# Layer 3 of a graph network: transposing node features on VectorE in 32 by 32 squares instead of on TensorE

## Chip, cores and metric

The kernel runs on one core of one Trainium2 chip. The metric is the time of one execution on the device in microseconds (us), the median of several runs. The core has five engines with a queue of instructions each: TensorE (PE in the profile; PEld is its loading of weights), VectorE (DVE), ScalarE (ACT), GpSimd (POOL) and SyncE (SP, here the queue that starts the loads). Each engine works its own queue in order; between engines, an instruction waits on semaphores for what it needs.

## What is computed

A stack of four layers over a graph of 3,327 nodes with 64 features each, and one weighted adjacency matrix of 3,327 by 3,327, all in fp32. Every layer normalizes, applies relu and adds its result to x. Cut to what matters here:

```python
# layer 0: two gated graph cells       (two products with adj)
# layer 1: ranks of non-zero entries   (one product with a matrix made from adj)
# layer 2: w = adj * adj, three hops   (three products with adj squared)
h = jnp.maximum(_layernorm(x, axis=-1), 0.0)
x = x + _L3_gnn_ref(h, adj, L3_gnn_W)          # layer 3

def _L3_gnn_ref(user_embs, adj, W):
    x = user_embs
    for k in range(2):
        agg = adj @ x
        x = jnp.tanh(jnp.concatenate([agg, x], axis=1) @ W[k])
    return x
```

So each of the two hops of layer 3 multiplies two things with weights: the sum over neighbours `agg`, and the node's own features `x` that the hop began with.

## The kernel before

**Layout.** The nodes are padded to 3,328 = 2 x 13 x 128: two halves `s`, 13 blocks `b` of 128 nodes. They are worked in four chunks of 3, 3, 3 and 4 blocks (both halves of each), and chunks go in two groups: (0, 1) and (2, 3). Features exist in two forms. In node form (`y[k][c]`, a tile of 128 partitions by blocks, halves and 64 features) the nodes lie on the partitions; this form is the stationary operand of the products with the adjacency. In feature form (`both[c]`, 128 partitions by 2 halves and blocks x 128 nodes) the features lie on the partitions. Of `both[c]`, half `s` holds on one set of 64 partitions the sum over neighbours and on the other set, `upper(1 - s)`, the node's own features, so that one matmul with 128 rows of weights does the concatenated product of the reference.

**Propagation.** There are eight products with the adjacency, k = 0 to 7; layer 3 is k = 6 and 7. A unit (k, c, t) takes one tile `t` of the transposed adjacency (128 source nodes by all targets of a group) and adds its part to the sum of chunk c in PSUM: two matmuls at L517, each with two records in the profile, so four. For k = 3, 4, 5 the tile is squared first, two of three by ScalarE (L360) and one of three by VectorE (L362). The tiles come from HBM into 20 slots on the SyncE queue (L325); a slot is loaded again when the last unit that uses its tile is done.

**Order.** The units are laid out in one list. `joint(g, k, ...)` runs products k and k + 1 of a group together, k + 1 some tiles behind; `alone` runs one. The end of the list is joint(1, 4), joint(0, 5), joint(1, 6), alone(0, 7). So source product 5 of chunks 2 and 3 ends in joint(1, 4), that of chunks 0 and 1 in joint(0, 5), and so on. `run` writes the units to the engines' queues in this order. Squares are issued up to three units before the unit that uses them (`EXPAND`).

**What comes between.** When the sum of a chunk is complete, its task starts: `after_5` to `after_7` in layer 3. A task is a Python generator. Each `yield us` says how much stream time should pass before its next part is put into the queues; `spend` counts that time down by 0.86 us per unit of 512 columns (0.645 us for 384). Each engine may run ahead of TensorE in its own queue as far as its data allow. If a chunk's next task begins, the rest of its old one is put out first (`finish`).

- `after_5(c)`: the sum of layer 2's last hop is copied (`evacuate`), multiplied with weights, added to x (L728), then layer norm and relu on VectorE with one power on GpSimd (L713 to L724). The result is y[6][c]. Then `transpose_to_features` puts the same features into `both[c]`.
- `after_6(c)`: `evacuate_stacked` copies the sum into the other half of `both[c]` (L704 on ScalarE, L705 on VectorE), `stacked_to_nodes` multiplies both parts with the weights (L677), tanh gives y[7][c], and `transpose_to_features` puts these into `both[c]` for the second hop.
- `after_7(c)`: the same without a transpose; the result is added to x and written out.

`transpose_to_features` takes a bank of PSUM, makes one matmul with the identity for each block and half (L694: 6 for three blocks and 8 for four; each stands in the profile as two records, so 12 and 16), and copies the bank out in two halves, here with `vector=True` one on ScalarE (L700) and one on VectorE (L698). It is also used once per chunk at the start, in `before_0`.

Of the kernel before, what the change touches and what calls it, by code (L numbers as in the profile page):

```python
# [44 lines left out]
N, D = 3327, 64  # L45
# [43 lines left out]
def upper(n):  # L89
    return slice(n * D, (n + 1) * D)  # L90
# [3 lines left out]
def kernel(  # L94
# [9 lines left out]
    nc = tc.nc  # L104
# [19 lines left out]
    both = [const.tile([P, 2, (b1 - b0) * P], F32, name=f"both{c}") for c, (b0, b1) in enumerate(CH)]  # L124
# [93 lines left out]
    def blocks(c):  # L218
        return CH[c][1] - CH[c][0]

    def width(c):
        return blocks(c) * P
# [15 lines left out]
    def take(sums=False, either=False):  # L238

        pool = idle_sums if sums else idle_temps  # L240
        if either and idle_sums and (not pool or released[idle_sums[0]] < released[pool[0]]):
            pool = idle_sums
        for c in list(tasks):
            if not pool and c not in running:
                advance(c)
        i = pool.popleft()
        return i, banks[i]

    def give(i):
        released[i] = max(released) + 1  # L250
        (idle_sums if i < 4 else idle_temps).append(i)

    def nodes(c):

        return feat.tile([P, blocks(c), 2, D], F32, name=f"y{c}")

    def flat(t):
        return t.rearrange("p b s d -> p b (s d)")
# [394 lines left out]
    def evacuate(acc, c, busy=False):  # L653
        m = work.tile([P, CWM], F32, name="t2")[:, :width(c)]
        if c % 2 or busy:
            nc.scalar.copy(m, acc[1][:, :width(c)])  # L656
        else:
            nc.vector.tensor_copy(m, acc[1][:, :width(c)])  # L658
        give(acc[0])
        return m  # L660

    def dense_to_nodes(ft, w, c):

        i, ps = take()
        v = view(ps, c)
        for b in range(blocks(c)):
            mm(v[:, b, :], ft[:, b * P:(b + 1) * P], bd[:, w - WL1, :])
        return i, v

    def stacked_to_nodes(c, w):  # L670

        i, ps = take()
        v = view(ps, c)
        for b in range(blocks(c)):
            for s in range(2):
                for n in range(2):
                    nc.tensor.matmul(v[upper(n), b, upper(s)], both[c][:, s, b * P + n * D:b * P + (n + 1) * D], w(s),  # L677
                                     start=True, stop=True)
        return i, v
# [7 lines left out]
                mm(v[:, b, upper(s)], ft[:, b * P:(b + 1) * P], ident[:, upper(1 - s)])  # L687
        return i, v

    def transpose_to_features(h, c, vector=False):  # L690
        i, ps = take()
        for b in range(blocks(c)):
            for s in range(2):
                nc.tensor.matmul(ps[upper(1 - s), b * P:(b + 1) * P], h[:, b, s, :], ident, start=True, stop=True)  # L694
        for s in range(2):
            u = upper(1 - s)
            if s and vector:
                nc.vector.tensor_copy(both[c][u, s], ps[u, :width(c)])  # L698
            else:
                nc.scalar.copy(both[c][u, s], ps[u, :width(c)])  # L700
        give(i)

    def evacuate_stacked(acc, c):
        nc.scalar.copy(both[c][upper(0), 0], acc[1][upper(0), :width(c)])  # L704
        nc.vector.tensor_copy(both[c][upper(1), 1], acc[1][upper(1), :width(c)])  # L705
        give(acc[0])

    def layernorm_relu(h, c, scale=None, pace=1.0):
        n = 2 * blocks(c)
        v = groups(xchunk(c))  # L710
        st = work.tile([P, 4, 8], F32, name="st", bufs=4)
        xc = work.tile([P, 8, D], F32, name="t2")
        nc.vector.tensor_reduce(st[:, 0, :n], v, AX.X, ALU.add)  # L713
        nc.vector.tensor_scalar(st[:, 1, :n], st[:, 0, :n], 1.0 / D, None, op0=ALU.mult)
        nc.vector.tensor_tensor(xc[:, :n], v, st[:, 1, :n, None].to_broadcast([P, n, D]), ALU.subtract)
        yield 1.5 * pace
        nc.vector.tensor_tensor(groups(h), xc[:, :n], xc[:, :n], ALU.mult)
        nc.vector.tensor_reduce(st[:, 2, :n], groups(h), AX.X, ALU.add)
        nc.vector.tensor_scalar(st[:, 2, :n], st[:, 2, :n], 1.0 / D, EPS, op0=ALU.mult, op1=ALU.add)  # L719
        nc.gpsimd.tensor_tensor(st[:, 3, :n], st[:, 2, :n], mhalf[:, :n], ALU.pow)  # L720
        yield 2.5 * pace
        if scale is not None:
            nc.vector.tensor_scalar(st[:, 3, :n], st[:, 3, :n], scale, None, op0=ALU.mult)
        nc.vector.scalar_tensor_tensor(groups(h), xc[:, :n], 0.0, st[:, 3, :n, None].to_broadcast([P, n, D]),  # L724
                                       op0=ALU.max, op1=ALU.mult)

    def residual(v, c):
        nc.vector.tensor_tensor(flat(xchunk(c)), flat(xchunk(c)), v[1], ALU.add)  # L728
        give(v[0])
# [73 lines left out]
    def before_0(c):  # L803
        h = nodes(c)
        yield from layernorm_relu(h, c)
        y[0][c] = h
        yield 12.0 + 3.0 * c
        transpose_to_features(h, c)
# [50 lines left out]
    def after_5(c, acc):  # L859
        m = evacuate(acc, c)  # L860
        yield 0.8
        v = dense_to_nodes(m, WL2 + 2, c)
        yield 0.8
        residual(v, c)
        yk = nodes(c)
        yield from layernorm_relu(yk, c)
        y[6][c] = yk
        yield 0.8
        transpose_to_features(yk, c, vector=True)

    def after_6(c, acc):
        evacuate_stacked(acc, c)
        yield 0.8
        v = stacked_to_nodes(c, lambda s: w3[:, 0, s])
        yk = nodes(c)
        nc.scalar.activation(flat(yk), v[1], AF.Tanh)
        give(v[0])
        y[7][c] = yk
        yield 1.2
        transpose_to_features(yk, c, vector=True)  # L880

    def after_7(c, acc):
        evacuate_stacked(acc, c)
# [8 lines left out]
        nc.scalar.dma_start(out=out[:, g0:g1], in_=xs[:, g0:g1])  # L892

    after[:] = [after_0, after_1, after_2, after_hop(3), after_hop(4), after_5, after_6, after_7]


# [60 lines left out]
```

## Time and profile before

| | |
|---|---|
| time, median of 3 runs (lowest, highest) | 737.91 us (737.57, 739.96) |
| span of the profiled execution | 734.9 us |
| read from HBM | 199.68 MB |
| granted clock of TensorE | 0.997 |
| products with the adjacency, fp32 (L517) | 2912 records, 536.0 us busy |
| squares on ScalarE (L360), on VectorE (L362) | 113.7 us, 69.4 us busy |

The busy time of an engine is the time in which at least one of its instructions ran. Matmuls overlap, so the mean length of one is more than the time by which the queue moves on; the step of the queue is seen in the chain of waits, where a run of matmuls stands with its start, its length and its count. The idle column of a group says how long the engine stood still just ahead of it, and for what.

### The profile page before, as it was taken

The page shows a single profiled execution, that of the slowest core. Times are in us where ns is not written, and L with a number is a line of the kernel's source. Part 1 is how long each engine was busy: PE and PEld are TensorE (multiplying, and loading weights), DVE is VectorE, ACT ScalarE, POOL GpSimd, SP SyncE. Part 2 cuts the span into 40 slices and gives each one's busy share as a digit, 9 for nine tenths or more (in the row PEclk, how much of TensorE's full clock was granted, in tenths as well). Part 3 has the DMA queues.
Part 4 walks back from the last instruction along what each step waited for, and adds up shares of the span by engine and source line. Part 5 has one row for each costly group of instructions (what it writes and reads, how often), then busy time and mean ns, then how long its engine had stood idle before and what let it go on. Part 6 is the DMA issues. An engine that isn't in the chain of part 4 may idle for free. (4 is left out here: it accounts for less than half of the span.)

```text
span 734.9 us, 12499 instructions
## 1 busy us (share of the span) xinstructions
PE 694.7 (95%) x5112; PEld 347.6 (47%) x5112; DVE 340.1 (46%) x599; ACT 244.6 (33%) x383; POOL 72.6 (10%) x105
## 2 busy tenths in 40 slices
PE   5988999899999898989899999999999999999997
PEld 2543566344546685545344444334344454344443
DVE  6656736434997978758764114321252520000101
ACT  0103100212037767768848213730044601000101
POOL 4100000001290502112200000000110000000000
PEclk9999999999999999999999999999999999999999
DMA  9999996189587365571799749953987399916991
GB/s 340 401 357 405 405 392 213 44 323 364 179 288 280 105 219 186 183 283 45 276 351 383 263 145 408 406 230 109 393 298 251 126 396 405 401 39 238 399 403 38
DMA packets 68964, 201.54 MB, mean 274 GB/s; under 512 B 7388, under 2 KB 8644, under 8 KB 68908
## 3 DMA queue, kind: packets, MB, share of 16 engines
q1 hardware_dynamic: 66156, 199.70, 73.2%
q8 instruction: 40, 0.66, 0.4%
q10 hardware_dynamic: 576, 0.85, 0.3%
q0 software_dynamic: 2176, 0.20, 0.2%
q14 instruction: 16, 0.13, 0.0%
HBM read 199.68 MB, written 0.85 MB: 273 GB/s over the span
## 5 line engine op out<-in xcount | busy, mean ns | idle before, releaser
L517 PE MATMUL sum<-adj,y 128*64 128x384 f32 (+1 forms) x2912 | 536.0, 516 | 17.8 <-DMA adj<-in_adjT 13.5
L517 PEld LDWEIGHTS sum<-adj,y 128*64 128x64 f32 x2912 | 218.4, 138 | 274.0 <-issue 230.3
L360 ACT ACTIVATE adj<-adj 128x768 f32<-128x768 f32 (+1 forms) x138 | 113.7, 891 | 57.7 <-PE sum L517 36.6
L383 DVE TENSOR_SCALAR adj<-adj 128x768 bf16<-128x768 f32 (+3 forms) x208 | 112.5, 593 | 33.5 <-PE temp L453 29.5
L362 DVE TENSOR_TENSOR adj<-adj 128x768 f32<-128x768 f32 (+1 forms) x70 | 69.4, 1022 | 57.1 <-DMA adj<-in_adjT 32.6
L433 ACT ACTIVATE e<-temp,bitsb 128x384 int16<-128x384 f32 (+1 forms) x123 | 68.8, 600 | 24.2 <-PE temp L229 18.4
L517 PE MATMUL sum<-e,adj 128*64 128x384 bf16 (+1 forms) x624 | 72.9, 339 | 0.0
L705 DVE COPY both<-sum 64x384 f32<-64x384 f32 (+1 forms) x16 | 9.5, 594 | 130.5 <-ACT both L704 130.5
L704 ACT COPY both<-sum 64x384 f32<-64x384 f32 (+1 forms) x16 | 8.0, 499 | 149.4 <-PE sum L517 149.4
L229 PE MATMUL temp<-adj,tri 128*64 128x384 bf16 (+1 forms) x320 | 49.6, 346 | 7.9 <-DMA adj<-totals 2.5
L720 POOL TENSOR_TENSOR st<-st,mhalf 128x6 f32<-128x6 f32 (+1 forms) x16 | 27.0, 1688 | 301.1 <-DVE st L719 292.6
L517 PEld LDWEIGHTS <-adj 128*64 128x64 bf16 x624 | 41.3, 110 | 17.2 <-issue 5.3
L388 POOL DMA_DIRECT2D adj<-totals x52 | 31.4, 606 | 134.6 <-DVE adj L768 74.7
L229 PEld LDWEIGHTS <-tri 128*64 128x64 bf16 x416 | 28.6, 111 | 29.2 <-issue 14.7
L431 DVE TENSOR_SCALAR e<-temp 128x512 int16<-128x512 f32 (+1 forms) x37 | 23.5, 634 | 20.5 <-PE temp L229 11.4
L748 PE MATMUL temp<-both,cells 128*64 128x384 f32 (+1 forms) x128 | 27.4, 521 | 4.1 <-DVE adj L757 2.2
L658 DVE COPY t<-sum 128x384 f32<-128x384 f32 x8 | 4.4, 556 | 54.3 <-PE sum L517 54.3
L453 PE MATMUL temp<-adj,behind 128*64 128x384 bf16 x208 | 28.6, 339 | 0.3 <-DVE adj L383 0.2
L656 ACT COPY t<-sum 128x384 f32<-128x384 f32 (+1 forms) x8 | 4.3, 533 | 67.0 <-PE sum L517 67.0
L700 ACT COPY both<-temp 64x384 f32<-64x384 f32 (+1 forms) x16 | 8.0, 502 | 55.5 <-PE temp L694 55.4
L453 PEld LDWEIGHTS <-behind 128*64 128x64 bf16 x208 | 16.2, 110 | 16.2 <-issue 14.4
L229 PE MATMUL sum<-adj,tri 128*64 128x384 bf16 (+1 forms) x96 | 17.4, 335 | 2.4 <-DVE e L431 2.4
(83 smaller groups left out, 293.5 us busy)
## 6 DMA issues: line engine op xcount, KB each, us to landing
adj<-in_adjT SPq DMA_DIRECT2D x130, 768.0 KB, 7.7
adj<-in_adjT SPq DMA_DIRECT2D x104, 896.0 KB, 11.6
xs<-in_x SPq DMA_DIRECT2D x1, 640.0 KB
out<-xs ACTq DMA_DIRECT2D x3, 192.0 KB, 1.9
adj<-totals POOLq DMA_DIRECT2D x26, 3.0 KB, 4.6
adj<-totals POOLq DMA_DIRECT2D x26, 3.5 KB, 2.2
folds<-in_weights SPq DMA_DIRECT2D x4, 64.0 KB, 11.8
out<-xs ACTq DMA_DIRECT2D x1, 256.0 KB
```

Of the source, the lines that this page charges most:

```text
L229: nc.tensor.matmul(out[hs], lhsT[:, hs], rhs, start=start, stop=stop)
L360: nc.scalar.activation(sq, v, AF.Square)
L362: nc.vector.tensor_tensor(sq, v, v, ALU.mult)
L383: nc.vector.tensor_scalar(t.mask.view[:rows, half], t.view()[:rows, half], 0.0, None, op0=ALU.not_equal)
L388: nc.gpsimd.dma_start(out=t.mask.view[P - 1:P], in_=totals[t.g][t.q:t.q + D + 1:D, :])
L431: nc.vector.tensor_scalar(wide[:, s], ps[:, :w], BITS, 0.0, op0=ALU.add, op1=ALU.max)
L433: nc.scalar.activation(wide[:, s], ps[:, :w], AF.Relu, bias=bitsb)
L453: nc.tensor.matmul(counts[c][1][s * D:(s + 1) * D, :w], behind[:, NQ - 1 - t.q:NQ - 1 - t.q + D], t.mask.view[:, s, t.cols(c)], start=firs ...
L517: nc.tensor.matmul(acc[h * D:(h + 1) * D, :w], yq[h], rhs[h], start=first and n == 0, stop=last and n == len(terms) - 1)
L705: nc.vector.tensor_copy(both[c][upper(1), 1], acc[1][upper(1), :width(c)])
L720: nc.gpsimd.tensor_tensor(st[:, 3, :n], st[:, 2, :n], mhalf[:, :n], ALU.pow)
L748: nc.tensor.matmul(ps[upper(1 - s), :w], cells[:, cell, s, g, :], both[c][:, s], start=True, stop=True)
```

## The change

The features of layer 3 no longer pass through TensorE and PSUM on their way into `both[c]`. VectorE has an instruction that transposes squares of 32 by 32. The new `transpose_on_vector` uses it from the node form in SBUF straight to the feature form in SBUF: for each half `s`, each quarter `q` of 32 nodes of a block and each half `f` of the 64 features, one instruction takes 32 partitions and all blocks of the chunk (3 or 4 squares). That is 16 instructions per chunk, put into the queue four at a time with `yield 1.5` after each four. The `yield` ahead becomes 1.5 as well (0.8 in `after_5`, 1.2 in `after_6` before). The start of the kernel (`before_0`) keeps the old way, with both copies on ScalarE as before. The purpose is to take the transposes and their weight loads off TensorE, and the copies out of PSUM off ScalarE and VectorE.

```diff
-    def transpose_to_features(h, c, vector=False):
+    def transpose_to_features(h, c):
...
-            u = upper(1 - s)
-            if s and vector:
-                nc.vector.tensor_copy(both[c][u, s], ps[u, :width(c)])
-            else:
-                nc.scalar.copy(both[c][u, s], ps[u, :width(c)])
+            nc.scalar.copy(both[c][upper(1 - s), s], ps[upper(1 - s), :width(c)])
         give(i)
+
+    def transpose_on_vector(h, c):
+
+        for s in range(2):
+            to = both[c][:, s].rearrange("p (b q n) -> p b q n", q=4, n=32)
+            for q in range(4):
+                for f in range(2):
+                    at = (1 - s) * D + f * 32
+                    nc.vector.transpose(to[at:at + 32, :, q], h[q * 32:(q + 1) * 32, :, s, f * 32:(f + 1) * 32])
+                if q % 2:
+                    yield 1.5
...
         y[6][c] = yk
-        yield 0.8
-        transpose_to_features(yk, c, vector=True)
+        yield 1.5
+        yield from transpose_on_vector(yk, c)
...
         y[7][c] = yk
-        yield 1.2
-        transpose_to_features(yk, c, vector=True)
+        yield 1.5
+        yield from transpose_on_vector(yk, c)
```

## The prediction

> **What bounds the kernel now.** I read the page's busy shares first, then the chain that ended last, the timeline of TensorE and VectorE around the lines that change, and the waits.
>
> ```profile
> PE 694.7 (95%) x5112; PEld 347.6 (47%) x5112; DVE 340.1 (46%) x599; ACT 244.6 (33%) x383; POOL 72.6 (10%) x105
> ```
>
> ```profile
> 588.99 0.66 PE temp L694 x12
> 589.64 5.16 PE sum L517 x32
> 594.80 0.66 PE temp L694 x12
> 595.46 9.67 PE sum L517 x60
> ```
>
> TensorE (PE) is busy for 95% of the span (first fence, the page). In the chain (second fence: start, length, what) the transposes of L694 stand between the big matmuls of L517 with no gap on either side: twelve take 0.66 us of TensorE's queue. So in layer 3 TensorE's queue sets the time, and whatever leaves it ends the program sooner, unless something else arrives late.
>
> ```profile
> L694 PE MATMUL temp<-ident,y 128*64 128x128 f32 x104 | 7.1, 275 | 1.4 <-DVE y L724 1.4
> ...
> L698 DVE COPY both<-temp 64x384 f32<-64x384 f32 x6 | 3.3, 550 | 14.6 <-ACT both L700 14.5
> ```
>
> These are groups from 500 to 735 us, shapes kept apart: 104 records of transposes (two for each matmul, 8 visits of a chunk), with 1.4 us of TensorE standing idle in front of them, waiting for VectorE's last step of the layer norm. The record of one is 275 ns long, but they overlap; their step is 0.66/12 = 55 ns.
>
> ```profile
> 533.31 0.88 PE L694 MATMUL temp<-ident,y 128*64 128x128 f32 x12 [0.16 <-DVE y L724]
> ...
> 544.75 1.09 PE L694 MATMUL temp<-ident,y 128*64 128x128 f32 x16 [1.19 <-DVE y L724]
> ...
> 548.11 32.47 PE L517 MATMUL sum<-adj,y 128*64 128x384 f32 x200 [0.33 <-DVE adj L362]
> ```
>
> In TensorE's timeline the idle time sits before the transposes of chunks 2 and 3; after the second, TensorE waits 0.33 us for a square of the adjacency (L362). The reason is seen on VectorE:
>
> ```profile
> 544.01 0.69 DVE L724 SCALAR_TENSOR_TENSOR y<-t,st 128x512 f32<-128x512 f32 x1 [1.53 <-POOL st L720]
> 546.51 0.68 DVE L698 COPY both<-temp 64x512 f32<-64x512 f32 x1 [1.81 <-ACT both L700]
> 547.12 0.94 DVE L362 TENSOR_TENSOR adj<-adj 128x768 f32<-128x768 f32 x1
> ```
>
> The square at 547.12 stood in the queue behind the copy L698, which itself waited for TensorE and ScalarE.
>
> [...] No transpose by VectorE is in the trace of before[...]. [...] So I let the transposes pay their full length one after the other. [...]
>
> **Part by part.**
>
> *Removed from TensorE.* Six visits with three blocks (12 matmuls, 0.66 us each in the chain) and two with four blocks (16 matmuls, 0.88 us: "667.25 to 668.13"): 6 x 0.66 + 2 x 0.88 = 5.7 us. The wait in front of them, 0.16 + 1.19 = 1.35 us (1.4 in the group), goes too: what TensorE finds next are propagation units that don't need the new features. The square that came 0.33 us late is no longer behind L698. Sum: 7.1 us, all on the path.
>
> *Removed elsewhere.* Eight copies L700 on ScalarE (about 0.5 us), eight L698 on VectorE (6 x 0.55 + 2 x 0.68 = 4.7 us), and the PSUM bank taken for each. Neither engine is the bound; I count nothing.
>
> *Added on VectorE.* Per visit 2 (halves) x 4 (node quarters) x 2 (feature halves) = 16 transposes of 32 partitions by 96 elements (three blocks) or 128. Price: in the trace a VectorE step over 6 elements takes 172 ns (L719) and one over 384 takes 553 ns (L713); the straight line between them is 1.0 ns per element, so 96 elements give 262 ns and 128 give 294 ns. Lower end: 172 ns, the price of a step with almost no data. Upper end: streaming at half rate, 172 + 2 x 90 = 352 ns. I take 262 and 294. Sum: 96 x 0.262 + 32 x 0.294 = 34.6 us, against 4.7 removed. It is laid out in bursts of four (about 1.05 us), with 1.5 us of modelled stream between them.
>
> *Does it hide?* By stage:
> 1. Chunks 2 and 3 after source layer 5 (533 to 552 us). This is the tight place. From 533.3 to 546.5 VectorE has three squares (2.9 us), the layer norm of chunk 3 (4.5 us), and now 16 transposes of chunk 2 (4.2 us): 11.6 of 13.2 us. It fits, but a square may queue behind a burst. Four squares (three, and the one at 547) behind one burst each is at most 4 x 1.05 to 1.18, about 4.4 us, if TensorE needed each at once. But the squares are issued three units ahead (3 x 0.65 = 1.9 us), and before, a 3.3 us run of layer norm in that queue cost TensorE nothing. I take 1 us for all of them.
> 2. Chunks 0 and 1 (588 to 600 us). Last square at 582; the layer norm of chunk 1 may stand behind two bursts (2.1 us, less the 0.55 us copy), so its features come at about 595.6 instead of 594.07. TensorE needs them at about 600.0 (six units of 0.65 us before the sum that ends at 603.9), less the 1.3 us saved: 598.7. Hidden.
> 3. After source layer 6 (606 to 614 and 656 to 669 us). VectorE has nothing to do but the transposes and the copies L705. The first burst can run as soon as the tanh is there (606.4), ahead of the copy at 609.6; the others are queued behind it. Hidden, at most some tenths.
> 4. Who waits for the transposes: only the matmuls L677 of the next visit of that chunk, at 605, 610, 656, 665, 686, 694, 725 and 729 us, each at least 16 us after the features were ready. 16 x 0.29 = 4.7 us, plus three gaps, fits everywhere.
>
> *Transfers.* If TensorE is 7 us early, can the adjacency keep up? By windows of 5 us, the last loads end between 715 and 720:
>
> ```profile
> 710.00:715.00 5.00, 5.00 (x34) 2.17 (x32) 0.00 (x0) 0.00 (x0) 0.00 (x0) 1.00 1.03 402
> 715.00:720.00 5.00, 5.00 (x34) 2.28 (x32) 0.00 (x0) 0.00 (x0) 0.00 (x0) 1.00 0.46 178
> 720.00:725.00 5.00, 5.00 (x34) 2.17 (x32) 0.22 (x1) 0.47 (x1) 0.00 (x0) 1.00 0.01 3
> ```
>
> (columns: stretch, length, busy time of PE, PEld, DVE, ACT, POOL, granted clock, DMA share, GB/s). The DMA share of 0.46 puts the last landing near 717.5 to 719. The last tile is first used by the last unit of chunk 0's sum, which ends when its copy L704 starts at 724.3, so at about 723.6. That leaves 4.5 us even if no load moved. But these loads wait for slots that TensorE frees ("SPq L325 <- PE sum L517" is the longest wait of that queue), and all the savings lie before 668, about where this last run of loads starts; so the loads move with TensorE.
>
> Net: 7.1 - 1.0 = 6.1 us, 737.9 - 6.1 = 731.8.
>
> **The rivals.**
> - *VectorE's queue takes the gain back.* Squares stand behind bursts and TensorE waits for the full 4.4 us: 7.1 - 4.4 = 2.7, so 735.2, and up to no change if the layer norm of chunk 1 is late too. For it: 88% of VectorE's time is taken from 533 to 546, and TensorE already waits once for a square there. Against: it fits, and ScalarE makes two of three squares.
> - *The transposes cost far more than a copy of their size, and the kernel gets slower.* At 0.8 us each, three times my price: 12.8 + 7.4 = 20.2 us of work in the 13.2 us of stage 1, 7 us late; chunk 1's features at 594.07 + 8 x 0.8 - 0.55 = 599.9, 1.2 us late; its 16 transposes end near 588.2 + 3.6 + 32 x 0.8 = 617 where L677 wants them at 610, 7 us late. 15 us lost, 7.1 won: about 746. For it: [...]the data is four bytes wide, and the trace has no such operation. [...]
> - *The transfers hide part of it.* The last tile binds: 4.5 us, so 733.4. For it: the DMA engines are full from 680 to 715. Against: the slot releases above.
>
> **How the numbers follow.** My forecast 0.67, VectorE's queue 0.15, dear transposes 0.14, transfers 0.04. Faster by over 0.3% means under 735.7 us: the forecast, the transfers, and 0.06 of the queue case: 0.77. The rest of the queue case is within: 0.09. Dear transposes are slower: 0.14. The range goes from 730.0 (no new waits gives 730.8, and a little for cheaper transposes that let squares come earlier) to 737.0, which takes in the queue case; outside it are the dear transposes and a few hundredths.
>
> **What would show it.** Right: 104 fewer records at L694, no wait on L724 by TensorE after 530 us, 128 VectorE transposes of 0.25 to 0.30 us, TensorE's waits for L362 of about 1 us, TensorE's busy time lower by about 5 us. Wrong: transposes over 0.45 us; TensorE waiting for L362, L724 or the transposes for more than 3 us in sum; waits for the adjacency's DMA in the last 130 us.

## The result and the profile after

The changed kernel takes 732.14 us (731.31 to 733.61), the kernel before 738.62 us (737.57 to 741.0), six runs each. The ratio is 0.9908 with a 95% interval of 0.9889 to 0.9927: faster by 6.5 us, between 5.4 and 8.2, which is under 1% of the time. The forecast was 6.1 us less, 731.8.

The page after, the line of engines, and the groups from 500 to 735 us with shapes kept apart, for the transposes and the squares on VectorE (columns: count, busy us, mean ns, idle us in front and what ended it):

```profile
PE 690.0 (95%) x5008; PEld 344.3 (47%) x5008; DVE 370.7 (51%) x719; ACT 240.2 (33%) x375; POOL 73.1 (10%) x105
```

```profile
L706 DVE STREAM_TRANSPOSE both<-y 32x96 f32<-32x96 f32 x96 | 25.9, 270 | 5.1 <-ACT y L883 2.9
L362 DVE TENSOR_TENSOR adj<-adj 128x768 f32<-128x768 f32 x17 | 16.1, 957 | 17.4 <-PE sum L517 10.1 <-issue 4.9 <-ACT adj L360 2.1
L706 DVE STREAM_TRANSPOSE both<-y 32x128 f32<-32x128 f32 x32 | 9.7, 303 | 1.1 <-ACT y L883 0.6
```

TensorE has 104 records fewer (5112 before, 5008 now) and is busy 4.7 us less. VectorE is busy 30.6 us more: its 35.6 us of transposes run beside TensorE's stream, and most of them cost nothing there. In the chain (start, length, what), TensorE now runs from chunk 1's dense step after product 5 to the first weights of layer 3 without the two transposes between:

```profile
585.52 0.66 PE temp L229 x12
586.17 16.77 PE sum L517 x104
602.94 0.70 PE temp L677 x24
```

What was lost is in TensorE's waits from 480 us on (total, times, longest):

```profile
PE sum L517 <- DVE adj L362: 1.7, 2, 1.4
PE temp L677 <- DVE both L712: 0.7, 3, 0.3
PE temp L677 <- ACT both L711: 0.6, 1, 0.6
```

The wait for the layer norm in front of L694 (1.4 us) is gone, those for the copies (L712 and L711, which were L705 and L704) are 0.7 and 0.6 us as before, and the wait for squares (L362) has grown from 0.3 to 1.7 us. VectorE's queue shows why, with TensorE's below it:

```profile
540.44 1.10 DVE L706 STREAM_TRANSPOSE both<-y 32x96 f32<-32x96 f32 x4
541.58 0.69 DVE L724 TENSOR_TENSOR y<-t 128x512 f32<-128x512 f32 x1
542.30 0.69 DVE L725 TENSOR_REDUCE st<-y 128x8 f32<-128x512 f32 x1
543.02 0.17 DVE L726 TENSOR_SCALAR st<-st 128x8 f32<-128x8 f32 x1
543.13 0.96 DVE L362 TENSOR_TENSOR adj<-adj 128x768 f32<-128x768 f32 x1
```

```profile
544.14 2.80 PE L517 MATMUL sum<-adj,y 128*64 128x384 f32 x16 [1.41 <-DVE adj L362]
547.23 32.47 PE L517 MATMUL sum<-adj,y 128*64 128x384 f32 x200 [0.29 <-DVE adj L362]
579.53 0.82 PE L229 MATMUL temp<-bd,t 128*64 128x128 f32 x12
```

A burst of chunk 2's transposes and three steps of chunk 3's layer norm run back to back, and the square stands behind them. It ends at 544.09; TensorE goes on at 544.14 after 1.41 us of waiting.

The first 500 us of the program differ by some us from one execution to the next (S1, below, begins at 526.3 us before the change, at 526.9 after it and at 529.7 in the kernel without transposes), so a change of 1 us is better seen in layer 3 itself. The table divides it by starts of TensorE's groups, read from its timeline of each run. S1: from chunk 2's L229 after product 5 to chunk 0's L229 (here the squares are still made). S2: to chunk 0's L677 after product 6. S3: to chunk 2's L677 after product 6. S4: to chunk 2's L677 after product 7. S5: to the last visit's L677 (chunk 1).

```
starts of S1 to S5, and the end of S5, us
before    526.30  580.41  604.96  655.36  686.00  729.37
after     526.91  579.53  602.77  651.86  680.97  724.34

us                        S1      S2      S3      S4      S5     sum
before                  54.11   24.55   50.40   30.64   43.37  203.07
after                   52.62   23.24   49.09   29.11   43.37  197.43
after - before          -1.49   -1.31   -1.31   -1.53    0.00   -5.64
```

S2 and S3 each lose two visits of three blocks, 2 x 0.66 = 1.32; S4 loses one of three and one of four blocks, 0.66 + 0.88 = 1.54. The matmul time of the removed visits comes back almost to the hundredth. Only S1 gave less than it lost: two visits (1.54), the two waits in front of them (1.35) and the old wait for a square (0.33) are 3.2 us, and 1.49 came back.

### The profile page after: what moved, and what is told of

Same layout as the page of the kernel before. It is cut to its first block, busy times and chain, and to the rows that moved or that the text cites. A ratio compares the mean times of both kernels' runs of the same rounds, so it can differ in the third digit from the quotient of the medians.

```text
span 729.9 us, 12406 instructions
## 1 busy us (share of the span) xinstructions
PE 690.0 (95%) x5008; PEld 344.3 (47%) x5008; DVE 370.7 (51%) x719; ACT 240.2 (33%) x375; POOL 73.1 (10%) x105
## 4 chain that ended last, share of the span: by engine, by line
PE 52%; DVE 4%; DMA 2%; issue 1%; POOL 1%; ACT 1%; POOLq 0%; ACTq 0%; DVEq 0%
PE sum L517 48%; PE temp L229 3%; DMA adj<-totals 2%; DVE adj L383 1%; PE temp L677 1%; DVE adj L362 1%; DMA out<-xs 1%; POOL st L727 1%; DVE e L431 0%; DVE both L706 0%; DVE both L712 0%; ACT both L711 0%; DVE st L720 0%; DVE st L725 0%; DVE y L724 0%
## 5 line engine op out<-in xcount | busy, mean ns | idle before, releaser
L517 PE MATMUL sum<-adj,y 128*64 128x384 f32 (+1 forms) x2912 | 536.4, 517 | 18.7 <-DVE y L731 11.3
L517 PEld LDWEIGHTS sum<-adj,y 128*64 128x64 f32 x2912 | 220.3, 138 | 279.3 <-issue 233.1
L383 DVE TENSOR_SCALAR adj<-adj 128x768 bf16<-128x768 f32 (+3 forms) x208 | 112.4, 593 | 32.9 <-PE temp L453 28.9
L362 DVE TENSOR_TENSOR adj<-adj 128x768 f32<-128x768 f32 (+1 forms) x70 | 69.4, 1021 | 51.7 <-DMA adj<-in_adjT 34.3
L517 PE MATMUL sum<-e,adj 128*64 128x384 bf16 (+1 forms) x624 | 73.0, 339 | 0.0
L712 DVE COPY both<-sum 64x384 f32<-64x384 f32 (+1 forms) x16 | 9.5, 594 | 116.2 <-ACT both L711 116.2
L711 ACT COPY both<-sum 64x384 f32<-64x384 f32 (+1 forms) x16 | 8.0, 498 | 164.6 <-PE sum L517 159.0
L229 PE MATMUL temp<-adj,tri 128*64 128x384 bf16 (+1 forms) x320 | 49.9, 348 | 7.5 <-DMA adj<-totals 2.2
L517 PEld LDWEIGHTS <-adj 128*64 128x64 bf16 x624 | 41.5, 110 | 17.0 <-issue 5.3
L229 PEld LDWEIGHTS <-tri 128*64 128x64 bf16 x416 | 28.5, 110 | 28.8 <-issue 16.0
L706 DVE STREAM_TRANSPOSE both<-y 32x96 f32<-32x96 f32 (+1 forms) x128 | 35.6, 278 | 6.2 <-ACT y L883 3.5
L755 PE MATMUL temp<-both,cells 128*64 128x384 f32 (+1 forms) x128 | 27.4, 521 | 4.1 <-DVE adj L764 2.2
L453 PE MATMUL temp<-adj,behind 128*64 128x384 bf16 x208 | 29.0, 339 | 0.8 <-DVE adj L383 0.8
L453 PEld LDWEIGHTS <-behind 128*64 128x64 bf16 x208 | 16.8, 110 | 16.2 <-issue 14.1
L229 PE MATMUL sum<-adj,tri 128*64 128x384 bf16 (+1 forms) x96 | 17.4, 335 | 2.4 <-DVE e L431 2.4
```

Source lines behind the costliest of these rows:

```text
L229: nc.tensor.matmul(out[hs], lhsT[:, hs], rhs, start=start, stop=stop)
L362: nc.vector.tensor_tensor(sq, v, v, ALU.mult)
L383: nc.vector.tensor_scalar(t.mask.view[:rows, half], t.view()[:rows, half], 0.0, None, op0=ALU.not_equal)
L453: nc.tensor.matmul(counts[c][1][s * D:(s + 1) * D, :w], behind[:, NQ - 1 - t.q:NQ - 1 - t.q + D], t.mask.view[:, s, t.cols(c)], start=firs ...
L517: nc.tensor.matmul(acc[h * D:(h + 1) * D, :w], yq[h], rhs[h], start=first and n == 0, stop=last and n == len(terms) - 1)
L706: nc.vector.transpose(to[at:at + 32, :, q], h[q * 32:(q + 1) * 32, :, s, f * 32:(f + 1) * 32])
```

## The experiments

Every kernel below is the changed one with the edit shown, but for the last, which starts from the late version. `...` marks what is cut. Ratios are to the kernel before on the same chip.

### Late transposes for chunks 2 and 3

```diff
         y[6][c] = yk
-        yield 1.5
+        yield 85.0 if c in GROUPS[1] else 1.5
         yield from transpose_on_vector(yk, c)
```

> The transposes of chunks 2 and 3 after product 5 are put into VectorE's queue some 85 us later, where it has nothing to do; all else as changed. Theory A (bursts of transposes stand in front of a square of the adjacency, which is why TensorE waits 1.41 and 0.29 us for L362): both waits go or shrink to 0.3 us in sum, the stretch from the start of chunk 2's L229 after product 5 to the start of chunk 0's L229 falls from 52.6 us to about 51.2, the time from 732.1 to about 730.7. Theory B (the layer norm of chunk 3 alone makes the square late, since TensorE now arrives earlier): the wait stays above 1 us, the stretch at 52.6, the time at 732.1.

Measured: 730.02 us (729.03 to 731.08), ratio 0.9890 [0.9871, 0.9910]. S1 is 50.48 us, the others as after the change. TensorE's waits from 480 us on have no line for L362 any more:

```profile
PE temp L677 <- DVE both L712: 0.7, 3, 0.3
PE temp L677 <- ACT both L711: 0.6, 1, 0.6
```

and the 32 postponed transposes run in VectorE's timeline with chunk 0's and 1's in one stretch in which it had nothing else to do:

```profile
604.24 0.56 DVE L712 COPY both<-sum 64x384 f32<-64x384 f32 x1 [1.44 <-ACT both L711]
604.83 18.04 DVE L706 STREAM_TRANSPOSE both<-y 32x96 f32<-32x96 f32 x60
649.18 0.56 DVE L712 COPY both<-sum 64x384 f32<-64x384 f32 x1 [26.31 <-ACT both L711]
```

Theory A holds: the bursts made the square late, not the layer norm alone. S1 fell by 2.14 us, more than the 1.4 expected. This is the fastest version that computes everything. The interval of its ratio overlaps that of the changed kernel, so the gain over it is shown by the stretches, in one trace of each, and not by the times alone.

### No transposes at all

```diff
         y[6][c] = yk
         yield 1.5
-        yield from transpose_on_vector(yk, c)
...
         y[7][c] = yk
         yield 1.5
-        yield from transpose_on_vector(yk, c)
```

> No transposes in layer 3 at all, on either engine; the node's own features in the feature form are left as layer 0 left them, so this part of both hops is not computed. Shows what taking them off TensorE gives when VectorE pays nothing. Theory A: 5.7 us of matmuls and 1.4 us of waits go, and nothing else was lost to VectorE than 1.7 us: the stretch from chunk 2's L229 to chunk 0's at about 51.2 us, time about 730.7, the same as with late transposes. Rival (VectorE's 36 us of transposes also slow other steps of the path by contention): more than 2.5 us below 732.1, and below the late version by over 1 us.

Measured: 729.15 us (727.74 to 732.19), ratio 0.9883 [0.9860, 0.9906]. S1 to S5 are 50.48, 23.24, 49.08, 29.11, 43.37: the late version's to 0.01 us. By the medians the rival stands half met (3.0 us below the changed kernel, but only 0.9 below the late one, with overlapping intervals); the stretches decide against it. So in the late version VectorE's 36 us cost TensorE nothing in layer 3, by queue or by contention, and the changed kernel pays 52.62 - 50.48 = 2.14 us for them, all of it in S1. The waits for L362 show 1.7 us. An estimate from the three lines of TensorE above accounts for the rest: 200 records move the queue by 547.23 to 579.53, 0.16 us each, so the 16 records before the second wait move it by 2.58 us, but the last of them ends only after 2.80. The profile counts idle time from that end, so each wait costs some 0.2 us more than it shows.

### Half of the change each

```diff
         y[6][c] = yk
-        yield 1.5
-        yield from transpose_on_vector(yk, c)
+        yield 0.8
+        transpose_to_features(yk, c, vector=True)
```

gives the kernel in which only the visits after product 6 are changed; the same edit in `after_6` (with its `yield 1.2`) the one in which only those after product 5 are. `transpose_to_features` is that of before in both.

> Only the transposes after product 6 go to VectorE; those after product 5 stay on TensorE. Theory A (each visit gives its own matmul time, as TensorE's queue is the path): 3 x 0.66 + 0.88 = 2.9 us, so 738.6 - 2.9 = 735.7; from the first L677 of chunk 0 after product 6 to the last visit's L677 of chunk 1, 124.4 us in the kernel before, about 121.5. Rival (the gain is the vanished waits and the squares after product 5): no more than 1 us, time 737.6 or more.

> Only the transposes after product 5 go to VectorE; those after product 6 stay on TensorE. Theory A: 2.9 us of matmuls and 1.35 us of waits go, 1.4 us of new waits for squares come: 2.8 us, time about 735.8; from the start of chunk 2's L229 after product 5 to chunk 0's L677 after product 6, 78.7 us before, about 75.9. Rival (most of the gain is here): 5 us or more, time 733.5 or less.

Measured: 735.51 us (732.25 to 736.21), ratio 0.9954 [0.9936, 0.9973], for the visits after product 6 alone; 735.17 us (731.86 to 738.27), ratio 0.9954 [0.9943, 0.9966], for those after product 5 alone. The stretches part the two better than the times. By stretches the first has S1 and S2 of before (54.12, 24.55) and S3 and S4 of after (49.08, 29.11); the second the reverse (52.61, 23.24, 50.40, 30.64). The parts add: 1.32 + 1.53 = 2.85 and 1.50 + 1.31 = 2.81, which give 5.66 of 5.64. Both rivals fall.

### Every transpose twice

```diff
                     nc.vector.transpose(to[at:at + 32, :, q], ...)
+                    nc.vector.transpose(to[at:at + 32, :, q], ...)
```

> Every transpose on VectorE is issued twice (same result, twice the price), places as changed. Worked from the trace after the change. After product 5 of chunks 2 and 3: VectorE has 16 us of work in the 13.2 us from 533 to 546, so squares come later still: the stretch from chunk 2's L229 to chunk 0's, 52.6 us now, about 55. After product 5 of chunks 0 and 1: now the last of 32 transposes ends at 600.9, and the copy L712 of chunk 0's sum stands behind them in the queue at 602.2: a margin of 1.3 us. With 8.7 us more the copy ends near 610 where TensorE wants it at 602.8: about 7 us of waiting, which the prediction on record had overlooked (it had only the matmuls L677 wait for the transposes). Theory A (these two margins decide): 2.5 + 7, and 1 at chunk 3 after product 6: time about 742. Rival (twice the price is hidden except for the squares, as the prediction on record argued): 732.1 + 2.5 = 734.6.

Measured: 753.21 us (751.55 to 754.18), ratio 1.0194 [1.0173, 1.0215]: slower than before the change by 14 us, and 11 us above theory A. The rival (734.6) falls. TensorE's timeline (start, length, idle in front):

```profile
543.21 2.16 PE L517 MATMUL sum<-adj,y 128*64 128x384 f32 x12 [2.47 <-DVE adj L362]
547.97 10.30 PE L517 MATMUL sum<-adj,y 128*64 128x384 f32 x52 [2.60 <-DVE adj L362]
560.78 3.05 PE L517 MATMUL sum<-adj,y 128*64 128x384 f32 x12 [2.51 <-DVE adj L362]
564.39 25.16 PE L517 MATMUL sum<-adj,y 128*64 128x384 f32 x152 [0.56 <-DVE adj L362]
...
620.37 1.34 PE L677 MATMUL temp<-w,both 128*64 128x64 f32 x20 [7.45 <-DVE both L713]
621.49 5.17 PE L517 MATMUL sum<-adj,y 128*64 128x384 f32 x24
```

S3 is 9.08 us longer than after the change, with one wait of 7.45 us for the copy of chunk 0's sum (L713 here, L712 after the change); I had expected 7. S4 is 1.04 longer, as expected. S1 is 9.57 longer where I had expected 2.5. There the squares were late four times instead of twice: VectorE fell behind, its bursts lost the pauses between them, and the squares of the later units queued behind up to 24 transposes of chunk 3 (7.9 us without a gap). Both margins were real, and the one in S1 was smaller than the sum over its first 13 us had let me think.

Part of the loss is not waiting. After the 7.45 us the same 20 records of L677 take 1.34 us (0.80 after waits of 0.20 and 0.25 us) and the next 24 of L517 take 5.17 (4.26 after the change): some 1.5 us of S3. In S1, 12 records of L517 take 3.05 us after the third wait (2.51 us), and 2.16 after the first (2.47 us). In all the slower records make nearly 3 us of S1, by an estimate: S1 is 11.7 us longer than without transposes, the four waits show 8.1, and 0.2 beside each makes 0.8. TensorE's granted clock was 0.988 in the mean of this execution and 0.995 after the change, where it was 1.00 over the whole of S1 with its wait of 1.41 us; the mean does not show in which stretches it was lower. So the doubled transposes are not a pure measure of the queue.

### All sixteen in one run

```diff
-                if q % 2:
-                    yield 1.5
...
-        yield from transpose_on_vector(yk, c)
+        transpose_on_vector(yk, c)
```

> The 16 transposes of a visit are put into VectorE's queue in one run of 4.3 to 4.8 us, without the pauses between bursts of four. Theory A (how they are spread matters, since squares stand behind them): squares after product 5 of chunks 2 and 3 come up to 3 us late once per visit: the stretch from chunk 2's L229 to chunk 0's at 54 to 57 us against 52.6; elsewhere nothing or gains; time 734 to 736. Rival (VectorE runs ahead anyhow, the spreading does nothing): stretch within 0.5 us of 52.6, time 732.1.

Measured: 734.99 us (732.59 to 738.07), ratio 0.9960 [0.9939, 0.9982]. S1 is 53.75 us, 1.13 more than with bursts (I had expected 1.4 to 4.4), and S3 is 50.86, 1.77 more, where I had expected nothing. That the time lies in the expected 734 to 736 is luck: most of the loss came from elsewhere. In VectorE's timeline and TensorE's:

```profile
603.87 4.52 DVE L706 STREAM_TRANSPOSE both<-y 32x96 f32<-32x96 f32 x16 [1.47 <-ACT y L881]
608.42 0.56 DVE L710 COPY both<-sum 64x384 f32<-64x384 f32 x1
```

```profile
609.04 0.80 PE L677 MATMUL temp<-w,both 128*64 128x64 f32 x20 [1.56 <-DVE both L710]
```

Chunk 1's copy (L710 here) stands behind all 16 transposes of chunk 0, and TensorE waited 1.56 us for it. With bursts, only the first four were ahead of it in the queue. So the pauses are worth 2.9 us by stretches and by time (734.99 - 732.14), more of it after product 6 than at the squares.

### A copy instead of the transpose

```diff
-                    nc.vector.transpose(to[...], h[...])
+                    nc.vector.tensor_copy(to[...], h[...])
```

> Each transpose replaced by a plain copy of the same squares by VectorE (same partitions, same counts; squares are left untransposed, so the features in layer 3 are in wrong places). Measures what the transposing itself costs over moving 32 partitions by 96 or 128 elements. Theory A[...]: copies take 262 and 294 ns as read from the line through 172 and 553 ns, so the transpose's 270 and 303 have 8 ns of their own. Rival 1 (a copy of this size streams faster than a transpose): 215 to 230 ns. Rival 2 (what is paid is the change of partitions, and a copy costs over 280 ns).

Measured in the groups from 500 us on (one run, 733.88 us, too few for a comparison of times):

```profile
L706 DVE COPY both<-y 32x96 f32<-32x96 f32 x96 | 20.8, 216 | 5.1 <-ACT y L883 2.9
L706 DVE COPY both<-y 32x128 f32<-32x128 f32 x32 | 7.0, 219 | 1.3 <-ACT y L883 0.9
```

Rival 1 is right: a copy takes 216 and 219 ns, the transpose 270 and 303. The transpose grows by 33 ns for 32 elements more, 1.03 ns per element; the copy by 3 ns. The changed kernel's S1 with these cheaper steps is 52.19, only 0.43 less, and the square is still 1.2 us late: 54 ns less on each step of three blocks (84 on those of four) hardly moves the queue in front of the squares.

### The first layer's transposes as well

```diff
         yield 12.0 + 3.0 * c
-        transpose_to_features(h, c)
+        yield from transpose_on_vector(h, c)
```

on top of the late version.

> The late version, and the transposes of the first layer (before_0, 13 blocks, 52 records, 2.9 us of TensorE's queue) on VectorE as well. Theory A (the gain is only to be had where TensorE's queue is the path; in the first 60 us TensorE waits for loads of the adjacency with the DMA engines full): within 0.7 us of the late version, about 730. Rival (TensorE's queue counts everywhere): 2.9 us less, about 727.

Measured: 733.38 us (731.39 to 736.05), ratio 0.9930 [0.9907, 0.9952], 3.4 us above the late version by the medians (every run above every run of it, though the intervals of the ratios just overlap). Both theories fall: it isn't neutral, it costs. The windows from 20 to 60 us (length, then busy time and count of PE, PEld, DVE, ACT, POOL, granted clock, DMA share, GB/s), first of the late version, then of this one:

```profile
20.00:60.00 40.00, 37.03 (x297) 20.73 (x298) 23.08 (x50) 4.28 (x9) 1.87 (x6) 1.00 1.01 385
```

```profile
20.00:60.00 40.00, 30.25 (x213) 19.96 (x214) 37.45 (x109) 0.28 (x1) 2.01 (x6) 1.00 1.01 381
```

And TensorE's waits in that window, first the longest of the late version, then those of this one:

```profile
PE sum L517 <- DMA adj<-in_adjT: 2.4, 4, 1.1
```

```profile
PE temp L453 <- DVE adj L383: 8.7, 8, 2.4
PE sum L517 <- DMA adj<-in_adjT: 0.9, 1, 0.9
```

VectorE makes the masks of the adjacency here (L383), which TensorE counts (L453). Its 23.08 us of work and the 17.8 us of transposes that were added (48 of 0.27 and 16 of 0.30) come to 40.9 us for 40; it is busy for 37.45 of them and becomes the bound. TensorE waits 8.7 us for masks, and product 0's first gate matmul (L755) starts at 64.98 instead of 60.83; where S1 begins, the two traces are 2.4 us apart. Theory A looked at TensorE and the loads only, and TensorE did wait 2.4 us for loads in this window; it missed that a third engine became slower than both.

## Why the prediction held, step by step

- *Removed from TensorE.* The mechanism is right: S2, S3 and S4 gave 1.31, 1.31 and 1.53 for 1.32, 1.32 and 1.54. The size is low: what was removed came to 7.8 us when nothing was added (203.07 less the sum over S1 to S5 without transposes, 195.28), against 7.1 worked out. The prediction names the square that came 0.33 us late as gone, but its sum of 7.1 holds only 5.7 and 1.35; with it, 7.4. The last 0.4 fits the estimate of 0.2 us beside each shown wait.
- *Price of a transpose.* 262 and 294 ns were the author's estimate, from the line between two rows of before; 270 and 303 were measured, with 1.03 ns per element between the two sizes. Nothing measured before spoke against a dearer one. Each quarter of the nodes goes to all four sets of 32 partitions, and all 128 transposes lie between 258 and 308 ns over both sizes.
- *Each paid in full.* An assumption that no trace of before could show. Right: four take 1.12 us. Where the next one writes makes no difference that shows: with every transpose issued twice, the second of a pair (L707) reads and writes just where the first (L706) did, and it starts no sooner after it (534.20 and 534.50 us) than the first of the next pair, which writes elsewhere, does after that (534.79).
- *New waits for squares.* Expected 1 us; 1.7 us in the waits, and 2.14 us in S1 by the run without transposes. This term was undersized by half. It should have been worked from the queue (which steps stand ahead of each square), not from the free time in 13 us.
- *Chunk 1's features after product 5.* Expected 1.5 us later, and hidden. From chunk 0's L229 to the end of that layer norm (L724 before, L731 after) it took 14.28 us instead of 13.66: 0.6 us later only, since a burst of 1.13 us ran while VectorE waited for GpSimd's power anyway (1.50 us of idle time there before, 0.34 after). Hidden.
- *Who waits for the transposes.* Overlooked. The prediction let only the matmuls L677 wait, with 16 us to spare; it saw the order of burst and copy after product 6, but not after product 5. There the copy of the next sum stands behind the transposes in VectorE's own queue. The last of them ended at 600.9 us, a margin of 1.3:

```profile
602.20 0.56 DVE L712 COPY both<-sum 64x384 f32<-64x384 f32 x1 [1.30 <-ACT both L711]
```

It held here, but by luck: the prediction had not worked it out. The doubled transposes and the single run showed what happens where it doesn't.

- *Transfers.* Right: no wait of TensorE for the adjacency after 480 us.
- *Sum.* 6.1 us expected; 5.64 by the stretches of the two traces, 6.5 by the medians. The gain was 0.7 us larger than worked out and the new waits 1.1 us larger; that the two errors pull in opposite ways is luck, and part of why the number is so near. The rival of dear transposes was worked out at 746 for three times the price; twice the number of transposes already gives 753, some 4 us of it, by the estimates above, in matmuls that ran slower after the waits. So that rival was undersized too, and it was the price that kept it away.

## What to carry to other kernels

When work leaves the engine whose queue sets the time, take as the gain the step by which that queue moves, not the length of the records (5.7 us here, where 104 records of 275 ns would make 28.6), and then look in the receiving engine's queue for what stands behind the new work: its copies and squares wait as if they needed it (TensorE then waited 1.41 us for a square, and 1.56 us for a copy behind all sixteen in one run). Short bursts with pauses limit that (2.9 us here), and a place where the engine has nothing to do takes it away wholly, if the consumer is far enough off; here that was worth another 2.1 us by the stretches. The same move costs time where the added work fills the receiving engine (3.4 us with the first layer's transposes): ask stage by stage, not once for the kernel.

## What was not expected of the hardware

A copy by VectorE of 32 partitions by 96 or 128 fp32 elements in SBUF takes 216 and 219 ns, nearly the same, where a transpose of the same squares takes 270 and 303. Two transposes one after the other start 0.28 us apart at 270 ns each (four take 1.12 us), so nothing of one hides in the other. In the kernel with doubled transposes, 20 matmul records took 1.34 us after a wait of 7.45 us, where they take 0.80 after 0.20, and 12 took 3.05 us after a wait of 2.51 us, so there a wait cost more than its length; after the first wait, of 2.47 us, it didn't: 12 records took 2.16.
